# Output layer of a graph-network kernel: four stages a unit apart, two buffers each, bias on GpSimd, last bins first

## The chip, the cores and the metric

The kernel runs on one core of a Trainium2 chip. A core has TensorE (PE, with its weight loads as PEld), VectorE (DVE), ScalarE (ACT), GpSimd (POOL) and SyncE (SP, which here only starts transfers); each takes its instructions in order from a queue of its own. The metric is the device time of one execution in microseconds, smaller is better. `L569` is line 569 of the kernel before the change.

## The reference, cut to what matters

```python
def smu(x, alpha=0.01, mu=2.5):
    return ((1 + alpha) * x + (1 - alpha) * x * erf(mu * (1 - alpha) * x)) / 2

# x (12500, 128), 400000 edges; src is sorted; W_f1 (128, 20), the other weights 128x128
h   = maximum(layernorm(x), 0)
h   = h @ W_in2f.T
Wij = smu(edge_attr_20 @ W_f1.T + b_f1) @ W_f2.T + b_f2        # one row per edge
Wij = Wij * edge_weight[:, None]
agg = segment_sum(h[dst] * Wij, src, num_segments=12500)        # (12500, 128)
out = x + smu(agg @ W_o1.T + b_o1) @ W_o2.T + b_o2              # the output layer
```

## The kernel before

The 12500 nodes are cut into `NB` = 98 bins of 128 rows; the last bin has 84. The edges go through the edge loop in groups of four tiles of 128: filter (two matmuls and a Gelu), gather of `h`, product, and a scatter (L572, GpSimd's indirect DMA) of each edge's message into a buffer in DRAM with room for every bin. The groups are divided into nine epochs with a buffer each. While epoch k is scattered, the buffer of epoch k-1 is read back and summed: `fetch` (L593) loads a chunk of `SPAN[k]` bins into a tile `rw` of 128 x (12 x 129) values, `choose` (L604) makes one-hot matrices `se` from the slot numbers that ride along, `add` (L617) multiplies them on TensorE into a PSUM bank `pg` of four bins, and L630 adds the bank to `agg`, which stays in SBUF, 128 x 12544. Four chunks are fetched ahead (`AHEAD`), in four buffers.

The last epoch has no edge loop beside it. Its buffer, 98 bins of 256 rows, is read in chunks of six bins (`SPAN` = 6, two matmuls a bin) after the last scatter has landed. Around its sums the output layer is computed in 26 units: 24 of four bins, then bin 96 and the 84 rows of bin 97 alone. A unit goes through

- `half`: L228 or L230 loads the unit's old rows of `x` (tile `hg`, 256 KB) from ScalarE's queue; L231 is the first matmul (PSUM `pu`, one bank); L232 the Gelu on ScalarE (`ge`); L233 on VectorE makes `sm` from both;
- `rest`: L239 is the second matmul (PSUM `pw`, one bank, four matmuls of 128 x 128); L240 adds the old rows into `ms`; L241 adds the output bias `bo2`, broadcast over the unit's bins, and L243 or L245 stores `ms` from ScalarE's queue.

The order on PE, DVE, ACT and SP is the order in which the program emits instructions. `half` of a unit is emitted when the four bins behind it have been added (`open_halves`, one unit of delay), and `rest` two bins later (`close_halves`). After the last bin, the remaining three units run one after another. At the end a flag (`nbad`, L830 to L835) is read by all engines; it decides whether a general path, not run here, computes the result anew.

The functions that the change touches, as they were:

Of the kernel before, what the change touches and what calls it, by code (L numbers as in the profile page):

```python
# [9 lines left out]
F32 = mybir.dt.float32  # L10
# [9 lines left out]
P = 128  # L20
# [9 lines left out]
GRP = 4  # L30
# [3 lines left out]
ROW = P + 1  # L34
# [5 lines left out]
def gnn_kernel(  # L40
# [19 lines left out]
    nc = tc.nc  # L60
# [15 lines left out]
    for n in PARTS:  # L76
        n = min(n, left)
# [5 lines left out]
    EPOCHS = len(eps_of)  # L83
# [6 lines left out]
    Q = [c // P for c in CAP]  # L90
    ROWS = 2 * max(Q)
    SPAN = [ROWS // q for q in Q]
# [46 lines left out]
    agg = const.tile([P, NB * P], F32, name="agg")  # L139
# [8 lines left out]
    w_o1 = const.tile([P, P], F32, name="w_o1")  # L148
    w_o2 = const.tile([P, P], F32, name="w_o2")
    bo2 = const.tile([P, P], F32, name="bo2")  # L150
# [69 lines left out]

    units = [(b, n, P) for b, n in chunks(NB - 1, GRP)] + [(NB - 1, 1, LASTB)]

    def half(unit, tiles, po, queue):
        xr, ge, sm, ys = tiles
        b, n, rows = unit
        w = (n - 1) * P + rows
        if rows == P:
            queue.dma_start(xr[:, :n, :], bin_rows(x, b, n))  # L228
        else:
            queue.dma_start(xr[:rows, 0, :], x[b * P:N, :])  # L230
        nc.tensor.matmul(po[:, :w], w_o1, agg[:, b * P:b * P + w], start=True, stop=True)  # L231
        nc.scalar.activation(ge[:, :w], po[:, :w], AF.Gelu, scale=ZS, bias=bz)  # L232
        nc.vector.scalar_tensor_tensor(sm[:, :w], po[:, :w], LIN, ge[:, :w], op0=ALU.mult, op1=ALU.add)  # L233

    def rest(unit, tiles, py, queue):
        xr, ge, sm, ys = tiles
        b, n, rows = unit
        for j in range(n):
            nc.tensor.matmul(py[:rows, j, :], sm[:, j * P:j * P + rows], w_o2, start=True, stop=True)  # L239
        nc.vector.tensor_add(ys[:rows, :n], py[:rows, :n], xr[:rows, :n, :])  # L240
        nc.vector.tensor_add(ys[:rows, :n], ys[:rows, :n], bo2[:rows].unsqueeze(1).to_broadcast([rows, n, P]))  # L241
        if rows == P:
            queue.dma_start(bin_rows(out, b, n), ys[:, :n])  # L243
        else:
            queue.dma_start(out[b * P:N, :], ys[:rows, 0])  # L245


    with tc.tile_pool(name="ld", bufs=4) as ld, \
# [151 lines left out]
        last = {}  # L400
# [182 lines left out]

        rows_in, sel, pgs = {}, {}, {}

        def fetch(k, c):

            b = c * SPAN[k]
            if b >= NB:
                return  # L590
            n = min(SPAN[k], NB - b)
            rw = rowp.tile([P, ROWS, ROW], F32, name="rw")
            nc.sync.dma_start(rw[:, :n * Q[k]].rearrange("p (b q) r -> p b (q r)", b=n),  # L593
                              bufs[k][b * CAP[k]:(b + n) * CAP[k], :].rearrange("(b p q) r -> p b (q r)", b=n, p=P))
            rows_in[c] = rw

        def choose(k, c):

            b = c * SPAN[k]
            if b >= NB:  # L600
                return
            m = min(SPAN[k], NB - b) * Q[k]
            se = rowp.tile([P, ROWS, P], F32, name="se", bufs=2)
            nc.vector.tensor_tensor(se[:, :m], irow_ps.unsqueeze(1).to_broadcast([P, m, P]),  # L604
                                    rows_in[c][:, :m, P:P + 1].to_broadcast([P, m, P]), op=ALU.is_equal)
            sel[c] = se

        def add(k, b, q):

            g = b % GRP  # L610
            c, i = b // SPAN[k], b % SPAN[k]
            if q == 0 and g == 0:
                pgs[0] = ps2.tile([P, GRP, P], F32, name="pg")
            if q == 0 and i == 0:
                choose(k, c + 1)
            o = i * Q[k] + q
            nc.tensor.matmul(pgs[0][:, g, :], rows_in[c][:, o, 0:P], sel[c][:, o, :], start=(q == 0),  # L617
                             stop=(q == Q[k] - 1))
            if q < Q[k] - 1:
                return  # L620
            if i == SPAN[k] - 1 or b == NB - 1:
                rows_in.pop(c), sel.pop(c)
                fetch(k, c + AHEAD)
            if g == GRP - 1 or b == NB - 1:
                dst = agg[:, (b - g) * P:(b + 1) * P]
                src = pgs[0][:, :g + 1].rearrange("p b n -> p (b n)")
                if k == 0:
                    nc.vector.tensor_copy(dst, src)
                else:
                    nc.vector.tensor_add(dst, dst, src)  # L630

        AHEAD = 4

        def begin(k):
            for c in range(AHEAD):
                fetch(k, c)

        def parts(k, upto):
            nonlocal done
            while done < upto:  # L640
                add(k, *work[done])
                done += 1
# [90 lines left out]
        for g in range(NG):  # L733
            s = g // PER
            k = epoch[s]
            g0, ng = eps_of[k][0] * PER, min(eps_of[k][1] * PER, NG - eps_of[k][0] * PER)
            i = g - g0
# [46 lines left out]
            assert k == 0 or taken_steps == COUNT and next(h_steps, None) is None  # L784
        k = EPOCHS - 1
        begin(k)
        choose(k, 0)
        mids, ends = [], []
        units_in = {}
        for unit in units:  # L790
            units_in.setdefault(unit[0] // GRP, []).append(unit)

        def open_halves(last):
            while mids and (last or len(mids) > 1):
                for unit in units_in[mids.pop(0)]:
                    tiles = (edge.tile([P, GRP * P], F32, name="hg").rearrange("p (b d) -> p b d", b=GRP),
                             edge.tile([P, GRP * P], F32, name="ge"),
                             edge.tile([P, GRP * P], F32, name="sm"),
                             msg.tile([P, GRP, ROW], F32, name="ms")[:, :, 0:P])
                    half(unit, tiles, ps1.tile([P, GRP * P], F32, name="pu"), nc.scalar)  # L800
                    ends.append((unit, tiles))
                    if last:
                        close_halves()

        def close_halves():
            while ends:
                unit, tiles = ends.pop(0)
                rest(unit, tiles, ps1.tile([P, GRP, P], F32, name="pw"), nc.scalar)

        for b in range(NB):  # L810
            for q in range(Q[k]):
                add(k, b, q)
            if b % GRP == 1:
                close_halves()
            if b % GRP == GRP - 1 or b == NB - 1:
                mids.append(b // GRP)
                open_halves(False)
        close_halves()
        open_halves(True)

    with tc.tile_pool(name="fps", bufs=1, space=PSUM) as fps:
        ends = const.tile([P, 2], F32, name="ends")
# [13 lines left out]
    with tc.If(flag > 0):  # L836
        with tc.tile_pool(name="gl", bufs=1) as gl, tc.tile_pool(name="gps", bufs=1, space=PSUM) as gps:
# [11 lines left out]
            with tc.For_i(0, NT, 1) as t:  # L849
# [11 lines left out]
                hg = gl.tile([P, D], F32, name="ghg")  # L861
# [39 lines left out]
            for b, n in chunks(NB, GRP):  # L901
                pt = gps.tile([P, GRP * P], F32, name="gpt")
                w = min(N, (b + n) * P) - b * P
                for j in range(n):
                    rows = min(P, N - (b + j) * P)
# [3 lines left out]
                nc.vector.tensor_copy(agg[:, b * P:b * P + w], pt[:, :w])  # L909
        with tc.tile_pool(name="gfin", bufs=1) as fin, tc.tile_pool(name="gfps", bufs=1, space=PSUM) as fps:  # L910
            for unit in units:
                tiles = (fin.tile([P, GRP, P], F32, name="xr"), fin.tile([P, GRP * P], F32, name="fge"),
                         fin.tile([P, GRP * P], F32, name="fsm"), fin.tile([P, GRP, P], F32, name="ys"))
                half(unit, tiles, fps.tile([P, GRP * P], F32, name="gpo"), nc.sync)
                rest(unit, tiles, fps.tile([P, GRP, P], F32, name="gpy"), nc.sync)


# [46 lines left out]
```

## Time and profile before

| | |
|---|---|
| median of 3 runs | 4244.77 us (4242.52 to 4252.45) |
| profiled execution, its own time | 4248.45 us |
| its span in the trace | 4246.6 us, mean granted clock 0.969 |
| busy over the span | PE 3736.8 (88%), DVE 3220.9 (76%), POOL 3017.8 (71%), ACT 2830.2 (67%) |
| last scatter issued (L572) | 4068.9 us |
| first fetch of the last epoch issued (L593) | 4071.28 us |
| first Gelu of the output layer (L232) | 4085.23 us |
| last VectorE instruction (L241) | starts 4241.59 us |

Times in the profile's views are microseconds from the span's start. A group's row has its line, engine, operation, output and inputs with shapes, the count, busy time, mean ns of one, and after the bar the idle time of the engine before these instructions with what ended it. A wait for several things is put down to the one that came last; where the engine named had long been done, it was another. ACTq and SPq mark instructions that start a transfer. Matmuls in f32 appear as two instructions each.

### The profile page before, as it was taken

To read this page: it belongs to the slowest core of one execution; us is meant where nothing else is said; L and a number is where in the kernel's file an instruction comes from. 1 tells how busy PE (TensorE), PEld (TensorE's weight loads), DVE (VectorE), ACT (ScalarE), POOL (GpSimd) and SP (SyncE) were. 2 spreads that over 40 slices of the span, in tenths; PEclk is the share of its full clock that TensorE was granted. 3 is DMA by queue.
4 is the path that set the end of the run, shared out by engine and by line. 5 is a ranking of instruction groups with operands and counts; after the bars stand their busy time and mean duration, and the time that the engine had idled before them with its cause. 6 is when DMAs were issued, how large, how long until landed. Compare 5 with 4: busy or idle time off the path is not lost. (4 is left out here: it accounts for less than half of the span.)

```text
span 4246.6 us, 74532 instructions
## 1 busy us (share of the span) xinstructions
PE 3736.8 (88%) x18497; PEld 2320.1 (55%) x18794; DVE 3220.9 (76%) x8578; ACT 2830.2 (67%) x11057; POOL 3017.8 (71%) x3133
## 2 busy tenths in 40 slices
PE   5877788999988999979998979998999799898976
PEld 2334434655555655546555546665666566565755
DVE  5886777877767877768877768887888688787865
ACT  4777777776666767657766757776777576676621
POOL 3777777777777777777777777777777777777620
PEclk9999999999999999989999989999999999999988
DMA  7855665766647666756666657775899699786754
GB/s 216 227 148 162 180 173 179 210 205 193 200 145 217 206 197 204 199 156 202 213 196 199 179 176 205 215 214 167 231 231 235 188 246 233 209 233 177 206 165 122
DMA packets 512380, 834.71 MB, mean 197 GB/s; under 512 B 84576, under 2 KB 323398, under 8 KB 511810
## 3 DMA queue, kind: packets, MB, share of 16 engines
q1 hardware_dynamic: 380986, 601.70, 51.8%
q0 software_dynamic: 100000, 206.60, 15.8%
q10 hardware_dynamic: 30952, 21.54, 1.8%
q8 instruction: 152, 2.49, 0.3%
q14 instruction: 290, 2.38, 0.2%
HBM read 456.16 MB, written 373.36 MB: 195 GB/s over the span
## 5 line engine op out<-in xcount | busy, mean ns | idle before, releaser
L572 POOL DMA_INDIRECT buf<-ms,ix x3125 | 3016.8, 965 | 1051.5 <-issue 249.2
L617 PEld LDWEIGHTS pg<-se,rw 128*128 128x128 f32 x8036 | 1096.5, 193 | 158.6 <-issue 21.2
L569 ACT ACTIVATE ms<-pt,w_sb 128x128 f32<-128x128 f32 x3125 | 905.1, 391 | 342.3 <-DMA buf<-ms,ix 163.6
L617 PE MATMUL pg<-se,rw 128*128 128x128 f32 x8036 | 1118.7, 276 | 10.4 <-DVE se L604 10.4
L467 ACT ACTIVATE jk<-pc,nbig 128x98 f32<-128x98 f32 x3125 | 1027.7, 351 | 6.1 <-PE pc L438 5.4
L539 PE MATMUL pw<-sm,w_f 128*128 128x512 f32 x1564 | 883.5, 647 | 40.6 <-DVE sm L505 35.4
L549 DVE SCALAR_TENSOR_TENSOR mt<-pw,b,hg 128x512 f32<-128x512 f32 x782 | 582.8, 745 | 348.2 <-ACT hg L528 345.9
L497 ACT ACTIVATE ge<-pu 128x512 f32<-128x512 f32 x782 | 468.4, 599 | 558.8 <-PE pu L489 537.0
L489 PE MATMUL pu<-f,w_f 128*128 128x512 f32 x1564 | 812.3, 601 | 4.2 <-DVE sm L505 4.1
L559 PE MATMUL pt<-ident,mt 128*128 128x128 f32 x3125 | 495.3, 281 | 298.8 <-DVE mt L549 295.8
L604 DVE TENSOR_TENSOR se<-irow_ps,rw 128x1536 f32<-128x1536 f32 (+1 forms) x345 | 587.5, 1703 | 145.8 <-DMA rw<-buf 125.2
L505 DVE SCALAR_TENSOR_TENSOR sm<-pu,ge 128x512 f32<-128x512 f32 x782 | 535.0, 684 | 209.7 <-ACT ge L497 200.8
L467 ACT ACTIVATION_READ_ACCUMULATOR jk<-pc,nbig 128x1 f32 x3125 | 674.5, 216 | 0.0
L528 ACT ACTIVATE hg<-ph 128x512 f32<-128x512 f32 x782 | 469.1, 600 | 305.3 <-PE ph L520 303.8
L520 PE MATMUL ph<-oh,hw 128*128 128x512 bf16 (+1 forms) x2049 | 631.8, 387 | 16.1 <-issue 0.4
L559 PEld LDWEIGHTS pt<-ident,mt 128*128 128x128 f32 x3125 | 352.9, 142 | 389.7 <-DVE mt L549 382.5
L424 DVE TENSOR_TENSOR co<-co,po 128x98 f16<-128x98 f16 x2353 | 502.6, 214 | 81.1
L520 PEld LDWEIGHTS <-hw 128*128 128x128 bf16 x2346 | 232.9, 99 | 553.6 <-issue 453.7
L410 DVE TENSOR_TENSOR po<-irow_ps,hi_b 128x392 f16<-128x392 f32 x782 | 433.1, 554 | 0.0
L539 PEld LDWEIGHTS pw<-sm,w_f 128*128 128x128 f32 x1564 | 236.8, 191 | 169.7 <-DVE sm L505 164.7
L489 PEld LDWEIGHTS pu<-f,w_f 128*128 128x128 f32 x1564 | 253.6, 196 | 27.9 <-DVE sm L505 5.6
L437 PE MATMUL pc<-co,ones_h 128*128 128x392 f16 x782 | 258.3, 330 | 3.5 <-DVE co L424 3.5
(104 smaller groups left out, 1702.0 us busy)
## 6 DMA issues: line engine op xcount, KB each, us to landing
rw<-buf SPq DMA_DIRECT2D x292, 774.0 KB
rbc<-rel_dram SPq DMA_DIRECT2D x390, 256.0 KB
buf<-zero SPq DMA_DIRECT2D x243, 387.0 KB
buf<-ms,ix POOLq DMA_INDIRECT x3125
buf<-zero SPq DMA_DIRECT2D x193, 258.0 KB
hw<-h_dram SPq DMA_DIRECT2D x391, 96.0 KB
rw<-buf SPq DMA_DIRECT2D x49, 645.0 KB
f<-in_f_t SPq DMA_DIRECT2D x390, 80.0 KB
```

The costliest lines, as they stand in the source:

```text
L424: nc.vector.tensor_add(co[:, j], co[:, j - 1], po[:, j - 1])
L467: nc.scalar.activation(jk, pc[:, j], AF.Relu, bias=nbig, accum_out=sl[:, j:j + 1])
L489: nc.tensor.matmul(pu[:, :n], w_f1, loaded[g // PER][0][:, o:o + n], start=True, stop=True)
L505: nc.vector.scalar_tensor_tensor(sm[:, :n], units_of.pop(g)[:, :n], LIN, hidden[g][:, :n], op0=ALU.mult, op1=ALU.add)
L520: nc.tensor.matmul(ph[:, :n], hw[:, q * D:(q + 1) * D], oh[:, o:o + n], start=(q == 0), stop=(q == 2))
L539: nc.tensor.matmul(pw[:, :n], w_f2, hidden.pop(g)[:, :n], start=True, stop=True)
L549: nc.vector.scalar_tensor_tensor(mt[:, :n], pws.pop(g)[:, :n], b2, rows_of.pop(g)[:, :n], op0=ALU.add, op1=ALU.mult)
L559: nc.tensor.transpose(pt[:, j, :], mt[:, j * P:(j + 1) * P], ident)
L569: nc.scalar.activation(ms[:, j, 0:P], pt[:, j], AF.Copy, scale=w_sb[:, t + j:t + j + 1])
L572: i = nc.gpsimd.indirect_dma_start(out=bufs[k][:, :], out_offset=bass.IndirectOffsetOnAxis(ap=ix[:, j:j + 1], axis=0), in_=ms[:, j, :], in ...
L604: nc.vector.tensor_tensor(se[:, :m], irow_ps.unsqueeze(1).to_broadcast([P, m, P]), rows_in[c][:, :m, P:P + 1].to_broadcast([P, m, P]), op= ...
L617: nc.tensor.matmul(pgs[0][:, g, :], rows_in[c][:, o, 0:P], sel[c][:, o, :], start=(q == 0), stop=(q == Q[k] - 1))
```

## The change

The output layer of the last epoch is cut into four steps that are emitted a unit or half a unit apart: `first_half` (first matmul and Gelu), `between` (`sm`), `second_half` (second matmul) and `store` (sum with the old rows, and the store). The matmul results take turns in two banks each, `pu`/`ph` and `pw`/`pt`, tiles that the edge loop has used. The old rows are loaded four units ahead, in turns into `hg` and `mt` with two buffers each, still from ScalarE's queue; GpSimd adds the output bias to them in place, and L241 is gone. The stores go into SP's queue, where the fetches are. The last chunk of bins (96 and 97) comes first in the last epoch, and the two small units with it; the order of the other epochs stays.

```diff
+    def with_bias(unit, xr, engine):
+        b, n, rows = unit
+        engine.tensor_add(xr[:rows, :n], xr[:rows, :n], bo2[:rows].unsqueeze(1).to_broadcast([rows, n, P]))
...
-    def rest(unit, tiles, py, queue):
-        xr, ge, sm, ys = tiles
+    def rest(unit, sm, py):
         b, n, rows = unit
         for j in range(n):
             nc.tensor.matmul(py[:rows, j, :], sm[:, j * P:j * P + rows], w_o2, start=True, stop=True)
+
+    def stored(unit, py, xr, ys, queue):
+        b, n, rows = unit
         nc.vector.tensor_add(ys[:rows, :n], py[:rows, :n], xr[:rows, :n, :])
-        nc.vector.tensor_add(ys[:rows, :n], ys[:rows, :n], bo2[:rows].unsqueeze(1).to_broadcast([rows, n, P]))
...
+        order_of = []
+        for k in range(EPOCHS):
+            cs = list(range(-(-NB // SPAN[k])))
+            order_of.append(cs if k < EPOCHS - 1 else cs[-1:] + cs[:-1])
...
-        mids, ends = [], []
...
+        small = [u for u in units if u[0] >= NB // GRP * GRP]
+        row_of, ready, opened, smoothed, summed = [], [], [], [], []
+        wanted = small + [u for u in units if u not in small]
+
+        def ask():
+            if wanted:
+                unit = wanted.pop(0)
+                name = ("hg", "mt")[len(wanted) % 2]
+                xr = edge.tile([P, GRP * P], F32, name=name).rearrange("p (b d) -> p b d", b=GRP)
+                old_rows(unit, xr, nc.scalar)
+                with_bias(unit, xr, nc.gpsimd)
+                row_of.append((unit, xr))
...
+        def first_half():
+            unit = ready.pop(0)
+            po = ps1.tile([P, GRP * P], F32, name=other(0, ("pu", "ph")))
+            ge = edge.tile([P, GRP * P], F32, name="ge")
+            half(unit, po, ge)
+            opened.append((unit, po, ge))
+
+        def between():
+            unit, po, ge = opened.pop(0)
+            sm = edge.tile([P, GRP * P], F32, name="sm")
+            bent(unit, po, ge, sm)
+            smoothed.append((unit, sm))
+
+        def second_half():
+            unit, sm = smoothed.pop(0)
+            py = ps1.tile([P, GRP, P], F32, name=other(1, ("pw", "pt")))
+            rest(unit, sm, py)
+            summed.append((unit, py))
+
+        def store():
+            unit, py = summed.pop(0)
+            was, xr = row_of.pop(0)
+            assert was == unit
+            stored(unit, py, xr, msg.tile([P, GRP, ROW], F32, name="ms")[:, :, 0:P], nc.sync)
+            ask()
+
+        for _ in range(4):
+            ask()
+        for c in order_of[k]:
+            for b in range(c * SPAN[k], min(NB, (c + 1) * SPAN[k])):
+                for q in range(Q[k]):
+                    add(k, b, q)
+                if b % GRP == 1:
+                    if opened:
+                        between()
+                    if summed:
+                        store()
+                if b % GRP == GRP - 1 or b == NB - 1:
+                    ready += [u for u in units if u[0] // GRP == b // GRP]
+                    if smoothed:
+                        second_half()
+                    if len(ready) > 1:
+                        first_half()
+        while ready or opened or smoothed or summed:
+            if smoothed:
+                second_half()
+            if ready:
+                first_half()
+            if opened:
+                between()
+            if summed:
+                store()
```

In the changed kernel the bias add on GpSimd is L236, the sum with the old rows L254, the first matmul, Gelu and `sm` are L240, L241 and L245, the second matmul L250, the stores L256 and L258, `choose` L627, the adds L640 and the sum into `agg` L653.

More of the change, by code (lines that the diff above doesn't have):

```diff
@@ L221, in gnn_kernel, with width, old_rows @@
     units = [(b, n, P) for b, n in chunks(NB - 1, GRP)] + [(NB - 1, 1, LASTB)]
-    def half(unit, tiles, po, queue):
-        xr, ge, sm, ys = tiles
+    def width(unit):
         b, n, rows = unit
-        w = (n - 1) * P + rows
+        return (n - 1) * P + rows
+    def old_rows(unit, xr, queue):
+        b, n, rows = unit
         if rows == P:
@@ L230, in half, with bent @@
             queue.dma_start(xr[:rows, 0, :], x[b * P:N, :])
-        nc.tensor.matmul(po[:, :w], w_o1, agg[:, b * P:b * P + w], start=True, stop=True)
+    def with_bias(unit, xr, engine):
+        b, n, rows = unit
+        engine.tensor_add(xr[:rows, :n], xr[:rows, :n], bo2[:rows].unsqueeze(1).to_broadcast([rows, n, P]))
+    def half(unit, po, ge):
+        w = width(unit)
+        nc.tensor.matmul(po[:, :w], w_o1, agg[:, unit[0] * P:unit[0] * P + w], start=True, stop=True)
         nc.scalar.activation(ge[:, :w], po[:, :w], AF.Gelu, scale=ZS, bias=bz)
+    def bent(unit, po, ge, sm):
+        w = width(unit)
         nc.vector.scalar_tensor_tensor(sm[:, :w], po[:, :w], LIN, ge[:, :w], op0=ALU.mult, op1=ALU.add)
-    def rest(unit, tiles, py, queue):
-        xr, ge, sm, ys = tiles
+    def rest(unit, sm, py):
         b, n, rows = unit
@@ L239, in rest @@
             nc.tensor.matmul(py[:rows, j, :], sm[:, j * P:j * P + rows], w_o2, start=True, stop=True)
+    def stored(unit, py, xr, ys, queue):
+        b, n, rows = unit
         nc.vector.tensor_add(ys[:rows, :n], py[:rows, :n], xr[:rows, :n, :])
-        nc.vector.tensor_add(ys[:rows, :n], ys[:rows, :n], bo2[:rows].unsqueeze(1).to_broadcast([rows, n, P]))
         if rows == P:
@@ L584, in gnn_kernel, with behind @@
         rows_in, sel, pgs = {}, {}, {}
+        order_of = []
+        for k in range(EPOCHS):
+            cs = list(range(-(-NB // SPAN[k])))
+            order_of.append(cs if k < EPOCHS - 1 else cs[-1:] + cs[:-1])
+        def behind(k, c, n):
+            i = order_of[k].index(c) + n
+            return order_of[k][i] if i < len(order_of[k]) else None
         def fetch(k, c):
+            if c is None:
+                return
             b = c * SPAN[k]
-            if b >= NB:
-                return
             n = min(SPAN[k], NB - b)
@@ L597, in choose @@
         def choose(k, c):
+            if c is None:
+                return
             b = c * SPAN[k]
-            if b >= NB:
-                return
             m = min(SPAN[k], NB - b) * Q[k]
@@ L614, in add @@
             if q == 0 and i == 0:
-                choose(k, c + 1)
+                choose(k, behind(k, c, 1))
             o = i * Q[k] + q
@@ L622, in add @@
                 rows_in.pop(c), sel.pop(c)
-                fetch(k, c + AHEAD)
+                fetch(k, behind(k, c, AHEAD))
             if g == GRP - 1 or b == NB - 1:
@@ L634, in begin @@
         def begin(k):
-            for c in range(AHEAD):
+            for c in order_of[k][:AHEAD]:
                 fetch(k, c)
@@ L786, in gnn_kernel @@
         begin(k)
-        choose(k, 0)
-        mids, ends = [], []
[L789 to L819, printed above, removed]
+        choose(k, order_of[k][0])
@@ new lines, in gnn_kernel, with other @@
+        turns = [0, 0]
+        def other(i, names):
+            turns[i] += 1
+            return names[turns[i] % 2]
+        def first_half():
[9 more added lines that the diff above has]
+            smoothed.append((unit, sm))
@@ L911, in gnn_kernel @@
             for unit in units:
[L912 to L915, printed above, removed]
+                xr, ys = fin.tile([P, GRP, P], F32, name="xr"), fin.tile([P, GRP, P], F32, name="ys")
+                ge, sm = fin.tile([P, GRP * P], F32, name="fge"), fin.tile([P, GRP * P], F32, name="fsm")
+                po, py = fps.tile([P, GRP * P], F32, name="gpo"), fps.tile([P, GRP, P], F32, name="gpy")
+                old_rows(unit, xr, nc.sync)
+                with_bias(unit, xr, nc.vector)
+                half(unit, po, ge)
+                bent(unit, po, ge, sm)
+                rest(unit, sm, py)
+                stored(unit, py, xr, ys, nc.sync)
 def arrange(inputs):
```

## The prediction

> **What bounds the kernel now.** I read first the busy time by stretch, to find the stage that the change touches. Columns: stretch and length, then busy us of PE, PEld, DVE, ACT and POOL, the granted clock, DMA share, GB/s.
>
> ```profile
> 4040.00:4060.00 20.00, 19.72 (x129) 15.03 (x129) 17.08 (x37) 12.39 (x48) 14.47 (x16) 1.00 0.49 149
> 4060.00:4080.00 20.00, 8.69 (x63) 8.09 (x64) 7.31 (x17) 1.68 (x6) 7.67 (x8) 0.75 0.54 169
> 4140.00:4160.00 20.00, 14.10 (x81) 11.62 (x80) 11.33 (x14) 2.06 (x3) 0.00 (x0) 0.84 0.55 158
> ```
>
> Until 4060 the edge loop keeps TensorE at 98%. Its instruction order is the same in both kernels, so nothing before 4065 should move. From 4067 on there is only the last epoch with the output layer: 180 of the 4246.6 us, in which no engine is full, GpSimd is idle, the clock is 0.84 and the DMA share 0.55. No engine bounds this stage; a chain does. Next the groups and the waits of 4084 to 4232, where 24 full units run (23 inside for some lines):
>
> ```profile
> L617 PE MATMUL pg<-se,rw 128*128 128x128 f32 x363 | 53.6, 296 | 0.0
> L239 PE MATMUL pw<-w_o,sm 128*128 128x128 f32 x186 | 30.7, 315 | 47.2 <-DVE sm L233 47.2
> L604 DVE TENSOR_TENSOR se<-irow_ps,rw 128x1536 f32<-128x1536 f32 (+1 forms) x15 | 25.2, 1677 | 1.0 <-PE pg L617 1.0
> L233 DVE SCALAR_TENSOR_TENSOR sm<-pu,ge 128x512 f32<-128x512 f32 x24 | 16.6, 690 | 21.1 <-ACT ge L232 21.1
> L232 ACT ACTIVATE ge<-pu,bz 128x512 f32<-128x512 f32 x24 | 16.5, 687 | 148.9 <-DVE agg L630 83.7 <-PE pu L231 56.2 <-DVE se L604 4.5
> L630 DVE TENSOR_TENSOR agg<-agg,pg 128x512 f32<-128x512 f32 (+1 forms) x24 | 16.0, 666 | 0.0
> L241 DVE TENSOR_TENSOR ms<-ms,bo 128x512 f32<-128x512 f32 x23 | 15.9, 692 | 0.8
> L240 DVE TENSOR_TENSOR ms<-pw,hg 128x512 f32<-128x512 f32 x23 | 15.9, 691 | 40.3 <-DMA hg<-in_x 26.0 <-PE pw L239 14.3
> ```
>
> TensorE loses 47.2 us, all waiting for `sm`; `sm` waits for the Gelu `ge`; and `ge` names `agg` L630, which it does not read. What holds `ge` is seen in one unit of the timeline (start, duration, idle before):
>
> ```profile
> 4129.73 0.52 ACTq L228 DMA_DIRECT2D hg<-in_x  x1
> ...
> 4133.77 1.02 PE L231 MATMUL pu<-agg,w_o 128*128 128x512 f32 x2
> ...
> 4135.43 0.69 DVE L240 TENSOR_TENSOR ms<-pw,hg 128x512 f32<-128x512 f32 x1 [2.00 <-DMA hg<-in_x]
> 4136.15 0.69 DVE L241 TENSOR_TENSOR ms<-ms,bo 128x512 f32<-128x512 f32 x1
> ...
> 4136.88 0.39 ACTq L243 DMA_DIRECT2D out<-ms  x1
> 4137.31 0.52 ACTq L228 DMA_DIRECT2D hg<-in_x  x1
> 4137.93 0.69 ACT L232 ACTIVATE ge<-pu,bz 128x512 f32<-128x512 f32 x1 [6.89 <-DVE agg L630]
> 4138.65 0.69 DVE L233 SCALAR_TENSOR_TENSOR sm<-pu,ge 128x512 f32<-128x512 f32 x1 [1.21 <-ACT ge L232]
> ...
> 4139.49 2.05 PE L239 MATMUL pw<-w_o,sm 128*128 128x128 f32 x8 [3.80 <-DVE sm L233]
> ```
>
> ScalarE's queue is a loop: the load of the old rows, 5.7 us until L240 can use them, L240, L241, the store's issue behind L241, the next load, and only then the next `ge`, though `pu` was ready at 4134.79. That is 7.58 us from load to load (4129.73 to 4137.31). Other units take 5.4. From the second load (4089.84) to the 24th (4229.37) the mean is 139.5/22 = 6.34 us a unit. After the 3.8 us of idle the eight L239 take 2.05 us instead of 1.13: the idle also costs TensorE its clock.
>
> **The change, part by part.** Off the loop: the store leaves ScalarE's queue for SP's, the loads run four units ahead in two tiles of two buffers, the bias add L241 (0.69) leaves VectorE, and `pu`/`ph` and `pw`/`pt` give each matmul result two banks. No step waits for a transfer just issued any more. What sets the pace next?
>
> TensorE packed: start to start in the trace, second half 0.97 (4146.60 to 4147.57), eight adds 0.89 (to 4148.46), first half 0.86 (to 4149.32), eight adds 0.89: 3.61 us a unit at full clock.
>
> VectorE and the order: for three units (12 bins, two `choose`) it has 3 x (`sm` 0.69 + add 0.69 + `agg` 0.68) + 2 x 1.75 = 9.7 us, below 3 x 3.61 = 10.8, but in a fixed order. I step through it with the adds of a unit starting at 0, 0.04 for a hand-over and 0.2 for the matmul's drain. Unit B: adds from 3.61, `ge` 3.82 to 4.51, `sm` to 5.24, add to 5.95, `choose` to 7.72, `agg` to 8.42; its second half starts on time at 5.39. Unit C: adds from 7.22, `ge` done 8.12, `sm` 8.44 to 9.13, so the second half starts at 9.19 instead of 9.0. Next unit: `agg` to 10.54, `choose` to 12.31, `sm` to 13.02, the second half at 13.08 instead of 12.8. The cycle repeats after 11.3 us: 3.77 a unit.
>
> ScalarE: `ge` 0.69 and one load issue, 0.39 to 0.52, waiting for VectorE's add; in those steps it ends over 0.8 us before the next `ge` is due. SP takes 26 stores of some 0.39 = 10 us. SP waited 111.9 us for TensorE between 4070 and 4247, so the issue time is free; but a store waits there for L254, and a fetch stands behind it. A fetch is used by `choose` about two chunks (11.3 us) after its issue, and one VectorE instruction of delay doesn't use that up. Each transfer also waits for the eighth before it; eight are three units' worth, again 11.3 us. The longer waits are off the path unless DMA gets slow.
>
> DMA: 98 bins x 132 KB = 12.9 MB in, 6.4 MB old rows, 6.4 MB out. The four fetches alone ran at 99.8% share and 313 GB/s (4072 to 4080, start included). In 4084 to 4232 the old rows and stores used 28.1% of 148 us for 12.04 MB, 3.45 us a MB, and the rest 24.8% for 9.78 MB, 3.75. At these, 12.9 x 3.75 + 12.8 x 3.45 = 92.5 us of full DMA. The stage below lasts about 105 us: DMA hides, at 88% share against 55%. This is the thinnest cover in the sum; I add 4 us for it (0 to 20).
>
> GpSimd: 26 adds of 128x512 f32 in L236. No such row is in the trace. Nearest by shape: L241, 0.69 on VectorE; nearest on the engine: L572, 0.97. The Trainium skill (GPSIMD Engine Reference, section 3.1) speaks against this move: a two-input add there is priced 1.96 times VectorE's, 4497 ns at 2048 elements, some 6 us more at the first call of newly loaded code. I take 0.69 x 1.96 = 1.36 us, an estimate; unscaled 4.5 is the upper end. With 1.36 it sits in a unit of 3.77 and its load is issued four units ahead: 15 us, less 5.7 for landing. By trace or rule alike it costs nothing; at 4.5 it would set the pace: 25 x 4.5 = 113 us. The first four stand behind the last scatter (4068.9), and 6 us of loading would end before the first is wanted at about 4084.
>
> Ports: the same skill (SBUF — State Buffer, Who interferes with whom) says that a VectorE instruction with two SBUF inputs and a GpSimd one that reads SBUF block each other for the whole instruction. In the trace GpSimd does no adds, so no row shows it. Of the rows above only L241 reads two SBUF tiles, and it goes; the others read one PSUM and one SBUF tile. By the rule the sum stays; if they did block, 1.36 a unit on VectorE (3.23 busy) makes 4.6 a unit: +20 us.
>
> Last bins first, start: fetches still wait for the last scatter (4071.28). The two-bin chunk (258 KB) should land near 4074 rather than 4075.84; its adds run on a cold clock to 4076.3. `choose` of chunk 0 follows to about 4078.6, so the first full unit starts 1 us later than now (4077.70). Its 16 adds take 3.3 us cold (0.207 each, from 32 in 6.64), then the two small units and a half-warm unit: I put the third full unit at 4086.7. The last adds begin 21 units later, 4086.7 + 21 x 3.77 = 4165.9, and end at 4167.7.
>
> The end: in the same steps, `ge`, `sm`, second half and add of the last two units take 7.0 us to 4174.7. Now it is 4224.9 to 4241.9, 17.0, because three units, two of them small, go one after another. From the last VectorE instruction to the end of the span are 4.7 us now; the last store is 256 KB instead of 42, +0.8. SP reads the flag ahead of the last store; on SP a register read with its checks fits in the 0.97 us between the issues of L385 and L388, and the flag is ready 1 us early: 0 (up to 1).
>
> Sum: 4174.7 + 4.7 + 0.8 + 4 for DMA = 4184.2, against a span of 4246.6: -62.4. The execution's own time is 4248.45, 1.85 outside the span, so 4186.1 for one like it. The median of the runs is 4244.77, 3.7 lower: 4182.4, rounded 4183.
>
> **Rivals.** (1) DMA becomes the bound: 25 MB at 200 to 215 GB/s, like the busier slices of the edge loop, instead of 240: 117 to 125 us from 4072.8 and 2.4 to the end: span 4192 to 4201. For: 512-byte rows both ways and 88% share. Against: slices of 106 us at 246 GB/s, and four chunks of prefetch. VectorE would wait for `rw`, as L604 does only at 4075 now. (2) GpSimd and VectorE block each other: the +20 above, 4204, and up to 4215 with the DMA allowance doubled. (3) Slower than before: the add in L236 works by rows of the broadcast operand, four short pieces for one, each with the 0.97 of a GpSimd instruction plus 0.8 of work: 7.1 us a unit. Then 25 x 7.1 = 178 from 4070 and 7 to the end: 4255 span, +8. It decides above 6.7 us an add. Against: L241 takes the same broadcast at the plain price. (4) The change doesn't shorten the loop because `ge` still waits for a transfer: only if the loads aren't ahead; they are issued in ScalarE's order four units early. Then -17 + 7 at the end: 4237.
>
> **Numbers.** Engine pace as summed 0.58 (4176 to 4192); DMA 0.25 (4192 to 4204); blocking 0.08 (4204 to 4215); unchanged loop 0.04; GpSimd slow 0.05. About 0.3% (13 us) is what a measurement of this kernel can tell from no change. The first three are faster: 0.91; the loop case about same: 0.04; slower 0.05. The range takes the first three, with PE packed without waits (24 x 0.16 = 4 less, no DMA allowance) as lower end: spans of 4176 to 4215, medians 1.8 lower: 4174 to 4213.
>
> **What would show it.** Right: second half to second half near 3.8 us, clock 1.00 from 4090, `ge` released by its own matmul, no wait of L254 for POOL, DMA share near 0.85, last adds near 4168 and 7 us after them. Wrong: `choose` or L254 waiting for DMA, L236 above 3.8 us, VectorE rows longer than 0.69 while GpSimd adds, a clock below 0.95, or the edge loop ending elsewhere than 4067.

## The result and the profile after

The changed kernel takes 4176.18 us, the median of 4 runs (4174.89 to 4181.54), against 4245.53 for the kernel before in the same comparison: ratio 0.9835, 95% interval [0.9822, 0.9848]. The prediction was 4183 in a range of 4174 to 4213. The profiled execution takes 4181.54, with a span of 4179.2 instead of 4246.6. One trace read below, that of e2, is of a slow execution (5317.66 us, against 5233.76 to 5272.49 for the others of e2), though the granted clock in the stage read from it is 1.00; the ratios are of fast executions alone.

The edge loop ends where it did. The first fetch of the last epoch is issued at 4071.5 (before: 4071.3), and from it to the end of the span are 107.7 us instead of 175.3: all of the difference lies in this stage. Busy time by stretch (stretch and length, busy us of PE, PEld, DVE, ACT and POOL, granted clock, DMA share, GB/s):

```profile
4060.00:4080.00 20.00, 9.53 (x65) 8.66 (x66) 7.47 (x19) 1.97 (x7) 10.94 (x12) 0.81 0.61 187
4100.00:4120.00 20.00, 20.00 (x143) 17.01 (x142) 16.08 (x20) 4.12 (x6) 7.65 (x6) 1.00 0.98 281
4140.00:4160.00 20.00, 20.00 (x143) 16.97 (x142) 16.08 (x21) 4.12 (x6) 7.64 (x6) 1.00 0.78 227
```

In 4140 to 4160 TensorE was busy for 14.10 of 20 us at a clock of 0.84; now it is busy for all of them at 1.00. The DMA share is up from 0.55 to 0.78, and to 0.98 in an earlier stretch, and TensorE has no idle time even there. The groups of 4084 to 4164 (busy us and mean ns of one, then idle us before it and its releasers):

```profile
L640 PE MATMUL pg<-se,rw 128*128 128x128 f32 x360 | 43.9, 275 | 0.0
L250 PE MATMUL pt<-w_o,sm 128*128 128x128 f32 x88 | 12.4, 284 | 0.0
L627 DVE TENSOR_TENSOR se<-irow_ps,rw 128x1536 f32<-128x1536 f32 x14 | 24.5, 1750 | 0.0
L245 DVE SCALAR_TENSOR_TENSOR sm<-pu,ge 128x512 f32<-128x512 f32 x11 | 7.6, 692 | 7.9 <-ACT ge L241 7.3
L241 ACT ACTIVATE ge<-pu,bz 128x512 f32<-128x512 f32 x11 | 7.6, 687 | 32.5 <-PE pu L240 32.5
L254 DVE TENSOR_TENSOR ms<-pt,mt 128x512 f32<-128x512 f32 (+1 forms) x11 | 7.1, 646 | 0.0
L236 POOL TENSOR_TENSOR mt<-mt,bo 128x512 f32<-128x512 f32 x11 | 14.0, 1275 | 40.3 <-DMA mt<-in_x 35.8 <-DVE se L627 2.7 <-DVE agg L653 1.0
```

The second matmul, which lost 47.2 us to `sm`, shows no idle time any more. The Gelu waits for its own matmul and no longer shows `agg`, which it does not read. `choose` (L627) and the sum (L254) have no idle time in front of them, so neither the fetches, nor the old rows, nor GpSimd's add is late. GpSimd itself waits 35.8 us for the old rows in this group; that is idle time of an engine with time to spare. The chain that ended last is TensorE alone until 4166.4 (start, duration, what):

```profile
4149.97 1.00 PE pw L250 x8
4150.97 0.86 PE ph L240 x2
4151.83 1.78 PE pg L640 x16
4153.61 1.00 PE pt L250 x8
```

1.00 + 0.86 + 1.78 = 3.64 us: that is the pace of a unit, and by this view all of it is TensorE's. The timeline shows a second limit at the same place (start, duration; in brackets the idle time before):

```profile
4131.61 1.13 PE L250 MATMUL pt<-w_o,sm 128*128 128x128 f32 x8
...
4132.57 1.02 PE L240 MATMUL pu<-agg,w_o 128*128 128x512 f32 x2
...
4133.70 0.69 ACT L241 ACTIVATE ge<-pu,bz 128x512 f32<-128x512 f32 x1 [2.96 <-PE pu L240]
4134.42 0.69 DVE L245 SCALAR_TENSOR_TENSOR sm<-pu,ge 128x512 f32<-128x512 f32 x1
4135.02 0.68 DVE L254 TENSOR_TENSOR ms<-pt,mt 128x512 f32<-128x512 f32 x1
...
4135.26 1.13 PE L250 MATMUL pw<-w_o,sm 128*128 128x128 f32 x8
...
4135.73 0.37 SPq L256 DMA_DIRECT2D out<-ms  x1
4135.74 0.47 ACTq L230 DMA_DIRECT2D mt<-in_x  x1
```

From one second half to the next are 3.65 us, and the steps between them touch: first half 0.96 later, Gelu 1.13 after it, `sm` 0.72 later, second half 0.84 after that. `sm` ends at 4135.11, 0.15 us before its matmul, and so in each of the 22 units from 4087 on. That is no slack: where TensorE is seen to wait for `sm`, as in e7 below with 0.41 us of idle time, its matmul also starts 0.15 us after `sm` ends. So TensorE is full, and the chain from one second half over the first half, the Gelu and `sm` to the next is just as long. In e3 below, 16 of 22 units follow each other at 3.58 or 3.59 us with the same matmuls, so TensorE's own work is some 0.06 us below the pace. The store and the next load are issued last, side by side on two queues, and neither TensorE nor VectorE waits for them.

### The profile page after: what moved, and what is told of

It reads as the page before. It is cut to its first block, busy times and chain, and to the rows that moved or that the text cites. A ratio compares the mean times of both kernels' runs of the same rounds, so it can differ in the third digit from the quotient of the medians.

```text
span 4179.2 us, 74603 instructions
## 1 busy us (share of the span) xinstructions
PE 3714.5 (89%) x18497; PEld 2304.1 (55%) x18794; DVE 3199.9 (77%) x8552; ACT 2828.3 (68%) x11057; POOL 3053.1 (73%) x3159
## 3 DMA queue, kind: packets, MB, share of 16 engines
q0 software_dynamic: 100000, 206.60, 16.1%
q14 instruction: 290, 2.38, 0.2%
## 5 line engine op out<-in xcount | busy, mean ns | idle before, releaser
L640 PEld LDWEIGHTS pg<-se,rw 128*128 128x128 f32 x8036 | 1087.7, 192 | 152.9 <-issue 14.4
L640 PE MATMUL pg<-se,rw 128*128 128x128 f32 x8036 | 1109.0, 275 | 7.9 <-DVE se L627 7.9
L627 DVE TENSOR_TENSOR se<-irow_ps,rw 128x1536 f32<-128x1536 f32 (+1 forms) x345 | 587.5, 1703 | 149.6 <-DMA rw<-buf 129.2
```

## The experiments

All numbers of a stage below are taken the same way: its length from the first fetch of the last epoch to the end of the span, and the mean time from one Gelu to the next over full units 2 to 23. e1 to e4 ran on one chip and e5 to e8 on another, and on both the whole program takes about 1 ms more (kernel before: 5287.61 and 5287.15 us); each ratio is to the kernel before on the same chip. There the executions of the kernel before alone lie between 5269.73 and 5320.59 us, so a time of one run prices nothing, and the prices below are differences between stages, from one trace each. The changed kernel was not traced on those chips. Its stage is set beside theirs because rows of the same shape last equally long (in e6 as here the Gelu 0.69, `choose` 1.75, GpSimd's add 1.27 us). Two stretches of the stage differ with edits that do not touch them: from the first fetch to the first add 3.6 us in the changed kernel and 5.4 in e5 and e8, from the end of the last VectorE instruction to the end of the span 8.0 in the changed kernel and 6.0 in e7 and e8. A difference of 2 us between two stages is therefore no price, and the time a unit is the surer reading.

| kernel | stage us | us a unit | time us | ratio to before |
|---|---|---|---|---|
| before | 175.3 | 6.40 | 4245.53 | |
| before, rows asked four ahead (e1) | 155.0 | 5.55 | 5278.82 | 0.9968 [0.9941, 0.9995] |
| before, stores in SP's queue (e2) | 136.0 | 4.84 | 5265.42 | 0.993 [0.9895, 0.9965] |
| changed, two steps as before (e4) | 131.0 | 4.59 | 5231.7 | 0.9887 [0.9836, 0.9938] |
| changed, one bank each (e5) | 123.8 | 4.18 | 5229.94 | one run |
| changed, rows one unit ahead (e3) | 116.4 | 3.89 | 5239.27 | 0.9876 [0.9832, 0.9919] |
| changed, bias on both engines (e8) | 116.2 | 3.99 | 5224.62 | one run |
| changed, bias on VectorE (e7) | 114.4 | 3.96 | 5271.97 | one run |
| changed, bins in order (e9) | 109.1 | 3.64 | 4178.12 | one run |
| **changed** | **107.7** | **3.65** | **4176.18** | **0.9835 [0.9822, 0.9848]** |
| changed, stores in ScalarE's queue (e6) | 106.6 | 3.69 | 5230.66 | one run |
| changed, warm start and other last stores (e10) | 104.8 | 3.65 | 4173.36 | 0.9829 [0.9816, 0.9843] |
| changed, four GpSimd adds a unit (e11) | 143.4 | 4.75 | 4216.66 | one run |

**One part alone, on the kernel before.** e1 takes the load out of the loop in ScalarE's queue, e2 the store.

```diff
 e1
+        for _ in range(4):
+            ask()                       # old rows into hg/mt, from nc.scalar
...
                 rest(unit, tiles, ps1.tile([P, GRP, P], F32, name="pw"), nc.scalar)
+                ask()
 e2
-                rest(unit, tiles, ps1.tile([P, GRP, P], F32, name="pw"), nc.scalar)
+                rest(unit, tiles, ps1.tile([P, GRP, P], F32, name="pw"), nc.sync)
```

> The kernel before with one edit: the old rows are loaded four units ahead into hg and mt, still from ScalarE's queue; stores, bias, banks, steps and order as before. Theory (the loop load, sum, bias, store issue, next load, Gelu on ScalarE's queue set the pace): the load leaves the loop, but the store still stands ahead of the next Gelu: second half 0.97, L240 and L241 to 2.4, store issue to 3.0, Gelu to 3.7, sm to 4.4 (5.4 where a choose comes first): about 4.8 us a unit instead of 6.3, span about 4210, the end (17 us from the last add) unchanged. Rival (the spacing of the steps is what costs, not the queue): pace stays above 5.8, span above 4234.

> The kernel before with one edit: the stores are started from SP's queue; loads, bias, banks, steps and order as before. Theory: with the store gone from ScalarE's queue, each load is started right behind the Gelu of the unit before, a unit early, by itself; pace 4.5 to 4.8, span about 4208, as with the rows ahead, since either edit opens the same loop. Rival (stores in SP's queue hold up the fetches): choose waits for rw, span above 4246. Rival (the spacing costs): span above 4234.

e1 came out at 5.55 us a unit, not at the 4.8 expected, and e2 at 4.84, just above its 4.5 to 4.8; that either edit opens the same loop is refuted. The timeline of e1 (its lines are numbered otherwise: L237 Gelu, L246 bias, L248 store, L226 load):

```profile
5161.99 0.69 DVE L246 TENSOR_TENSOR ms<-ms,bo 128x512 f32<-128x512 f32 x1
...
5162.72 0.39 ACTq L248 DMA_DIRECT2D out<-ms  x1
5163.15 0.52 ACTq L226 DMA_DIRECT2D hg<-in_x  x1
...
5163.77 0.69 ACT L237 ACTIVATE ge<-pu,bz 128x512 f32<-128x512 f32 x1 [4.79 <-PE pg L622]
...
5165.33 1.13 PE L244 MATMUL pw<-w_o,sm 128*128 128x128 f32 x8 [1.71 <-DVE sm L238]
```

The landing time is gone, the loop is not. The store still waits for the bias add of this unit, and behind the store stand the load's issue and the next unit's Gelu, although the Gelu's input was ready by about 5162.8 (L236 begins at 5161.71 and takes 1.02). One unit's sum is still ahead of the next unit's Gelu. In e2 it is not (L243 store, L228 load, L232 Gelu):

```profile
5230.98 0.37 SPq L243 DMA_DIRECT2D out<-ms  x1
5231.09 0.69 ACT L232 ACTIVATE ge<-pu,bz 128x512 f32<-128x512 f32 x1 [3.85 <-PE pu L231]
5231.17 0.37 ACTq L228 DMA_DIRECT2D hg<-in_x  x1
```

One word of the change opens the loop: the Gelu is released by its own matmul, and the load follows it a unit early, with no rows asked ahead. The stage falls by 175.3 - 136.0 = 39.3 us, twice what the loads alone bring (20.3). The times agree: 0.993 is 37 us, with an interval of 18 to 56, and for e1 it is 17 us, 3 to 31. What keeps e2 at 4.84 is for the most part the two-step order: from 5195 to 5295 TensorE still loses 21.5 us to `sm` (us in total, times, longest), and e4 below, which has all of the change but the four steps, stands at 4.59.

```profile
PE pw L239 <- DVE sm L233: 21.5, 20, 1.8
```

**The changed kernel with one part undone.** e4 goes back to two steps a unit (the Gelu and `sm` issued with the first matmul, the sum and the store with the second). e5 gives each matmul result one bank.

```diff
 e4                                                   # at b % GRP == 1
-                    if opened:
-                        between()
-                    if summed:
+                    if smoothed:
+                        second_half()
                         store()
...
-                    if smoothed:
-                        second_half()
                     if len(ready) > 1:
                         first_half()
+                        between()
 e5
-            po = ps1.tile([P, GRP * P], F32, name=other(0, ("pu", "ph")))
+            po = ps1.tile([P, GRP * P], F32, name="pu")
...
-            py = ps1.tile([P, GRP, P], F32, name=other(1, ("pw", "pt")))
+            py = ps1.tile([P, GRP, P], F32, name="pw")
```

> The changed kernel with one edit: the four steps are put back into the two of before (first half and sm together after the fourth bin, second half and store together after the second); queues, rows ahead, GpSimd bias, banks and order as changed. Theory: TensorE waits for sm again: first half ends 2.0 after the second half began, Gelu 2.9 to 3.6, sm to 4.3 or, behind a choose, 4.8: pace 4.4 to 4.6 instead of 3.65, span about 4201. Rival (only queues and prefetch matter): pace below 3.8, span 4179 to 4184.

> The changed kernel with one bank for each matmul result again (pu and pw only). Read by the stage from the last epoch's first fetch to the end (175.3 us before, 107.7 changed) and the pace of the Gelus (6.40, 3.65). Theory: pu in one bank costs nothing, since the first half of the next unit stands behind the second half, which needs sm; pw in one bank makes each second half wait for L254, which starts 0.6 after sm and ends 0.5 after the second half could begin: pace about 4.15, stage about 119. Rival (the banks are idle cover): pace 3.65, stage 108.

Both came out at the pace that was expected; the stage of e5, 123.8, is longer than the 119, and 1.8 us of that are a later first add. In e4 the waits of 5110 to 5205 (engine, tile and line, releaser, us in total, times, longest) name the step that is missing:

```profile
ACT ge L241 <- PE ph L240: 42.8, 11, 4.2
PEld pt L250 <- DVE sm L245: 9.8, 10, 1.2
PEld pw L250 <- DVE sm L245: 9.8, 10, 1.2
```

The Gelu is on time, but only eight adds stand between the first half and the second, and TensorE waits about 1 us for `sm` in every unit. The four steps are worth 131.0 - 107.7 = 23.3 us (19.7 of them from the second full Gelu to the 23rd), once the rest is there; alone on the kernel before they were not run. In e5 the second half waits for the sum of the unit before it, because it writes the bank that the sum reads:

```profile
5164.53 0.68 DVE L254 TENSOR_TENSOR ms<-pw,hg 128x512 f32<-128x512 f32 x1
...
5165.26 1.16 PE L250 MATMUL pw<-w_o,sm 128*128 128x128 f32 x8 [0.38 <-DVE ms L254]
```

That is 0.38 us of idle time 21 times, and 0.53 us a unit in all. The stage is 16.1 us longer, of which 11.2 lie in the same part (87.8 against 76.6): so much is shown for the second banks. Which of the two pairs it is was not tried apart; the waits name `pw`.

e3 asks for the rows of one unit at the start instead of four; e6 puts the stores back into ScalarE's queue; e9 leaves the bins in their order.

```diff
 e3
-        for _ in range(4):
-            ask()
+        ask()
 e6
-            stored(unit, py, xr, msg.tile([P, GRP, ROW], F32, name="ms")[:, :, 0:P], nc.sync)
+            stored(unit, py, xr, msg.tile([P, GRP, ROW], F32, name="ms")[:, :, 0:P], nc.scalar)
 e9
-        wanted = small + [u for u in units if u not in small]
+        wanted = list(units)
...
-            order_of.append(cs if k < EPOCHS - 1 else cs[-1:] + cs[:-1])
+            order_of.append(cs)
```

> The changed kernel with one edit: one unit's old rows asked for at the start instead of four, so that each load is issued only after the unit before has used its rows. Theory: a loop comes back, load to landing 5.2, GpSimd 1.27, sum 0.68, issue: 7.3 us a unit instead of 3.65, span about 4179 + 24 x 3.65 = 4267, slower than before, with the Gelu no longer waiting behind a store but the store step waiting for GpSimd. Rival (the steps and banks carry the gain): pace below 5, span below 4215.

> The changed kernel with the stores back in ScalarE's queue. Theory: in the four-step order the store's wait for L254 ends 1.4 us after a Gelu and the next Gelu is due 2.9 after it; store issue 0.4 and load issue 0.5 fit between: pace stays 3.65, and as SP is free of the last store the end after the last VectorE instruction falls from 8.0 towards 5: stage 104 to 108. Rival (a store in ScalarE's queue costs by itself, as the 39 us of the store edit alone suggest): pace 4.5 or more, stage 125 or more.

> The changed kernel with the bins of the last epoch in their natural order, the two small units last. Theory (the order is worth little: the first two bins and the two small units run for nothing while the first fetches land): the first full adds come 1 us earlier, but the end has two more steps of a chain, some 1.3 us each, and TensorE has some 2 us of adds and small matmuls more after 4079: stage 109 to 112 instead of 107.7, pace 3.65. Rival (no effect): 107 to 108.5.

The expectation of e3 fell. It had the loop come back at 7.3 us a unit; 3.89 was measured, and the kernel is still faster than before. In the timeline of e3:

```profile
5160.35 0.69 ACT L241 ACTIVATE ge<-ph,bz 128x512 f32<-128x512 f32 x1 [2.90 <-PE ph L240]
5160.41 0.37 ACTq L230 DMA_DIRECT2D mt<-in_x  x1
5160.56 0.69 DVE L254 TENSOR_TENSOR ms<-pt,mt 128x512 f32<-128x512 f32 x1 [2.38 <-POOL mt L236]
```

The load at 5160.41 does not wait for the sum at 5160.56 that stands ahead of it in the program, because with four buffers it overwrites nothing that is still to be read. It is issued right behind the Gelu, a unit early. Some units wait all the same, L254 here for 2.38 us: its own rows were asked for at 5153.25, 1.15 us behind a fetch, and GpSimd could start on them only at 5159.26. Asking four ahead is worth 116.4 - 107.7 = 8.7 us, 5.2 of them from the second full Gelu to the 23rd, and it is not what opens the loop.

e6 shows that the queue of the stores, which decides on 39 us in the kernel before, hardly matters any more: 106.6 us. The Gelu now stands a unit ahead of the store in the program, so the store at 5183.48 delays only the load at 5183.96, and the next Gelu is not due until 5185.08:

```profile
5183.48 0.39 ACTq L256 DMA_DIRECT2D out<-ms  x1
...
5183.96 0.47 ACTq L230 DMA_DIRECT2D hg<-in_x  x1
...
5185.08 0.69 ACT L241 ACTIVATE ge<-pu,bz 128x512 f32<-128x512 f32 x1 [2.96 <-PE pu L240]
```

The pace is 3.69 instead of 3.65 because two loads take 1.60 and 1.32 us to issue and hold up a Gelu each; the end behind the last VectorE instruction is 2.1 us shorter. So another queue and another order are alternatives for the loop, and of the two only the order can also close TensorE's gap, together with the second banks (e5) and the bias (e7). e9 is 1.4 us longer: its first full Gelu comes 1.6 us earlier after the fetch and its last VectorE instruction 2.1 us later, as expected in kind, and the end behind that is 0.7 us shorter. One trace each does not tell such a difference from none.

**The bias.** e7 puts it back on VectorE, as a second add behind the sum. e8 leaves GpSimd's add in place and has VectorE add zeros there, so that VectorE does an instruction with two SBUF inputs beside GpSimd's. e11 has GpSimd add zeros three times more.

```diff
 e7, e8                                               # bo2 in e7, zeros in e8
         nc.vector.tensor_add(ys[:rows, :n], py[:rows, :n], xr[:rows, :n, :])
+        nc.vector.tensor_add(ys[:rows, :n], ys[:rows, :n], bo2[:rows].unsqueeze(1).to_broadcast([rows, n, P]))
...
-                with_bias(unit, xr, nc.gpsimd)       # gone in e7 only
 e11
-        engine.tensor_add(xr[:rows, :n], xr[:rows, :n], bo2[:rows].unsqueeze(1).to_broadcast([rows, n, P]))
+        for more in (bo2, zero[:, 0:P], zero[:, 0:P], zero[:, 0:P]):
+            engine.tensor_add(xr[:rows, :n], xr[:rows, :n], more[:rows].unsqueeze(1).to_broadcast([rows, n, P]))
```

> The changed kernel with the bias added on VectorE behind L254, as before, and nothing on GpSimd. Theory: VectorE's instructions follow each other at 0.60 to 0.61 us, choose at 1.67: four of the one and two thirds of the other make 3.54 a unit, just under 3.65; pace 3.65 to 3.9, stage 108 to 114. Rival (relief of VectorE is a main part of the gain): pace 4.2 or more, stage above 121.

> The changed kernel, GpSimd's bias add kept, with one VectorE instruction more behind L254 that adds zeros (two SBUF inputs, shape of the old bias add). Theory (the two engines block each other where VectorE reads two SBUF tiles): the added rows that meet a GpSimd add last up to 0.69 + 1.27 = 2.0 us, or the GpSimd rows grow from 1.27 to as much; pace above that of the kernel with the bias on VectorE alone by 0.1 to 0.5. Rival (no blocking): rows stay at 0.69 and 1.27 whether they meet or not, and the pace is that of the kernel with the bias on VectorE.

> The changed kernel with three GpSimd adds of zeros more for each unit (four of 1.27 = 5.1 us instead of one). Theory (one add has cover up to the pace of 3.65, beyond it GpSimd sets the pace): pace 5.1 to 5.3, stage 107.7 + 24 x 1.5 = about 143, VectorE's rows unchanged at 0.68 to 0.69 as each reads one SBUF tile. Rival (the four units of rows ahead absorb it): pace 3.65 for most units, stage below 120.

e7 is a little slower than expected, 3.96 a unit: the longer row of VectorE instructions makes `sm` late (start, duration, idle time before):

```profile
5207.36 0.68 DVE L245 SCALAR_TENSOR_TENSOR sm<-pu,ge 128x512 f32<-128x512 f32 x1
...
5208.19 1.02 PE L250 MATMUL pw<-w_o,sm 128*128 128x128 f32 x7 [0.41 <-DVE sm L245]
```

The move to GpSimd is worth 6.7 us of the stage, 6.5 of them from the second full Gelu to the 23rd. e8 shows where the ports matter (L255 is the added instruction, L236 GpSimd's):

```profile
5164.77 0.69 DVE L255 TENSOR_TENSOR ms<-ms,zero 128x512 f32<-128x512 f32 x1
5164.78 1.82 POOL L236 TENSOR_TENSOR mt<-mt,bo 128x512 f32<-128x512 f32 x1 [1.44 <-DVE ms L254]
...
5175.15 1.27 POOL L236 TENSOR_TENSOR mt<-mt,bo 128x512 f32<-128x512 f32 x1 [4.91 <-DMA mt<-in_x]
5175.47 0.68 DVE L245 SCALAR_TENSOR_TENSOR sm<-pu,ge 128x512 f32<-128x512 f32 x1
...
5176.38 1.27 POOL L236 TENSOR_TENSOR hg<-hg,bo 128x512 f32<-128x512 f32 x1
...
5176.79 1.41 DVE L255 TENSOR_TENSOR ms<-ms,zero 128x512 f32<-128x512 f32 x1
```

At 5164.77 VectorE is first by 0.01 us, and GpSimd takes 1.82 instead of 1.27. At 5176.79 GpSimd has been at an add since 5176.38, and VectorE's 0.69 becomes 1.41. Of the 26 added instructions 10 meet a GpSimd add; six of the 10 are themselves longer, 0.82 to 1.41 us, and each of these ends 0.54 to 0.55 us after GpSimd's add; two make GpSimd's add longer; two overlap it by 0.15 us at most and change nothing. The `sm` at 5175.47 runs inside a GpSimd add and takes its usual 0.68: it reads one PSUM and one SBUF tile. That is the rule of the Trainium skill that the prediction weighed (SBUF — State Buffer, Who interferes with whom), now with its numbers. It costs little. The pace, 3.99, is 0.03 above that of e7 and not the 0.1 to 0.5 expected, and of the 1.8 us between the stages 1.7 lie before the first add.

e11 makes GpSimd the bound. The stage, 143.4, is what was expected; the mean pace of the Gelus, 4.75, is not, since the first units run ahead of GpSimd. Groups of 4090 to 4190, then waits of the same stretch:

```profile
L237 POOL TENSOR_TENSOR mt<-mt,zero 128x512 f32<-128x512 f32 x30 | 38.1, 1269 | 2.4
```

```profile
DVE ms L255 <- POOL hg L237: 15.9, 8, 2.6
DVE ms L255 <- POOL mt L237: 13.7, 7, 2.6
```

Four adds of 1.27 are 5.1 us a unit. The first seven units still run at 3.65, on the rows asked ahead; the rest take 5.26, as expected of all, and VectorE's sum waits for GpSimd. The kernel takes 4216.66 us, still less than before. In the changed kernel, one add of 1.27 in a unit of 3.65 leaves GpSimd idle for two thirds of it.

**A version beyond the change.** e10 takes two losses that the trace after still shows. TensorE stands idle for 7.9 us while the first fetch lands, and its clock is then 0.50 from 4074 to 4080, so eight matmuls into an unused tile keep it busy there; and the last three stores go to ScalarE's queue.

```diff
         choose(k, order_of[k][0])
+        for _ in range(8):
+            idle = ps1.tile([P, GRP * P], F32, name="pc")
+            nc.tensor.matmul(idle, ident, w_sb[:, 0:GRP * P], start=True, stop=True)
...
-            stored(unit, py, xr, msg.tile([P, GRP, ROW], F32, name="ms")[:, :, 0:P], nc.sync)
+            stored(unit, py, xr, msg.tile([P, GRP, ROW], F32, name="ms")[:, :, 0:P],
+                   nc.sync if len(row_of) > 2 else nc.scalar)
```

> The changed kernel with two additions: eight matmuls of constants into an unused bank (512 columns each) keep TensorE busy between the edge loop and the last epoch's first adds, and the last three stores go through ScalarE's queue, so that SP passes the flag's branch early. Theory: the first 16 full adds take 1.8 us instead of 3.4 (clock 1.00 instead of 0.5), and the end after the last VectorE instruction falls from 8.0 to about 6: stage 103.5 to 105 instead of 107.7, time 3 us (0.07%) below the changed kernel. Rival for the start (the first adds wait for fetch and choose anyway): 107.7 - 2 = 105.7. The adds' start stays within 0.3 us of 8.0 after the fetch.

The first 16 adds of a full unit, in the changed kernel and then in e10:

```profile
4079.46 3.43 PE L640 MATMUL pg<-se,rw 128*128 128x128 f32 x16
```

```profile
4064.17 9.31 PE L813 MATMUL pc<-w_sb,ident 128*128 128x512 f32 x16
4073.32 1.05 PE L640 MATMUL pg<-se,rw 128*128 128x128 f32 x8
...
4076.15 1.95 PE L640 MATMUL pg<-se,rw 128*128 128x128 f32 x16
```

They take 1.95 instead of 3.43 us, at a clock of 1.00. From the last VectorE instruction to the end of the span are 6.3 us instead of 8.0, though e7 and e8 end as early with their stores in SP's queue (see the end, below). The stage is 2.9 us shorter. The time, 4173.36, beats the kernel before clearly (0.9829); against the changed kernel the two intervals overlap, so the 2.9 us are shown by the trace and not by the times.

## Why the prediction was right, and which terms were off

The mechanism holds: the loop in ScalarE's queue opens, TensorE is full at full clock, and DMA, GpSimd and the ports stay hidden. The predicted span was 4184.2, the measured one is 4179.2. The median, 4176.18, lies at the lower end of the range and of the 4176 to 4192 that were given 0.58. Its terms:

| term | predicted | measured | difference |
|---|---|---|---|
| 21 units of the pace | 21 x 3.77 = 79.2 | 21 x 3.646 = 76.6 | -2.6 |
| allowance for DMA | 4 | 0 | -4.0 |
| adds of the third full unit begin | 4086.7 | 4086.0 | -0.7 |
| the last adds | 1.8 | 2.0 | +0.2 |
| end of the last adds to the end of the last VectorE instruction | 7.0 | 6.6 | -0.4 |
| from there to the end of the span | 5.5 | 8.0 | +2.5 |

They add up to -5.0: 7.7 us too much and 2.7 too little, so that a part of the nearness is luck. The rest of the 6.8 us between 4183 and 4176.18 comes from the way from the span to the median: the profiled execution stands 5.4 us above its median where the prediction took 3.7 (1.7 more), its time outside the span is 2.35 where it took 1.85 (0.5 less), and it rounded up by 0.6.

- **The pace.** The step that failed is VectorE's order. It was stepped through with durations, 0.69 and 1.75, plus a hand-over, and had `sm` 0.2 to 0.3 late in two of three units. In the trace two adjacent instructions start 0.60 apart (4134.42 and 4135.02): the next one starts before the last has ended. `sm` starts 0.03 us after its Gelu has ended in each of the 22 units, so VectorE's order delays nothing. The 0.04 us between TensorE's 3.61, which the paragraph before had, and the 3.65 measured fits the hand-over from `sm` to the second half. e7 shows that nothing was left over: one more instruction a unit, and `sm` is 0.41 late.
- **DMA.** The allowance of 4 us was not used. The share was 0.89 at 258 GB/s from 4084 to 4164, where 88% was predicted, and reached 0.98 at 281, and no `choose` in this stretch waited for rows. The first rival, DMA as the bound, had 200 to 215 GB/s for this; it fell on that number.
- **GpSimd.** The add was estimated at 1.36 us from the skill's ratio (GPSIMD Engine Reference, section 3.1) and measured at 1.27, 1.84 times VectorE's 0.69. The price read without scaling, 4.5, and the slow rival's 7.1 are far off. No 6 us of loading show either (that figure stands in section 2.1 of the page, not in 3.1): the first adds take 0.47, 0.46, 1.26 and 1.25 us.
- **Ports.** As argued, none of the rows that are left reads two SBUF tiles, and none is lengthened: `sm`, sum and `agg` take 0.68 to 0.69 and `choose` 1.75 whether GpSimd adds or not. e8 shows that the blocking is real for those that do.
- **The loop.** The prediction let the store, the loads four ahead and the bias leave the loop together, without a price for each. Apart, the store is worth 39.3 us (e2), the loads 20.3 (e1), and in the changed kernel the loads are worth 8.7 (e3) and the stores' queue next to nothing (e6). The rival in which the loop stays because the loads are not ahead is refuted by e3.
- **The end.** The last term, 4.7 + 0.8, was mis-sized by 2.5 us. SP does read the flag ahead of the last store, as was said; what the sum put at nothing is its branch over the fallback, which now stands behind that store. SP's waits on itself, of 4070 to 4180 (us in total, times, longest):

```profile
SPq L900 <- SPq L900: 5.3, 2, 3.3
```

The first lasts 3.3 us from the branch at 4171.6, the second 2.0 us, from 4175.1 to 4177.1. In the kernel before SP reached its branch at 4229.6, 17 us before the end of the span, so that whatever it takes there lay beside the last units. Of the two it is the second that counts: the last store lands at 4174.9, so SP could not have finished before that anyway. And the queue of the stores alone does not bring it about. e7 and e8 keep theirs in SP's queue, wait 3.3 us at the branch but not a second time, and end 6.0 us after their last VectorE instruction; the changed kernel, e3, e4, e5, e9 and e11 have the second wait, of 2.0 to 2.3 us. Why is open.

## What to carry to other kernels

Where an engine's first unit of idle time is put down to a tile that the instruction does not read, follow its queue in program order: here a store's issue held the next unit's Gelu, and either another queue for the store or an order with the Gelu ahead of it takes that away, while asking for inputs earlier does not. A chain of hand-overs between four engines is then shortened by giving each step its own place a stage apart and each result a second bank; step through it with the distances between starts, not with durations, and do not take the time of a hand-over for slack. What was hidden beside the old end of the program comes into view when that end moves up.

## What the hardware showed that was not expected

- The branch at the end. In the changed kernel VectorE stands from 4171.5 to 4174.9 and SP from 4171.6 to 4175.0 and again from 4175.1 to 4177.1. In the kernel before VectorE needed 0.6 us at the same place (4242.2 to 4242.8). In e6, without stores on SP, SP's first wait is 2.7 us and the end comes 5.9 us after the last VectorE instruction. In SP's second wait the only transfers in the trace are three of the kind `instruction`, on queues q8 and q14, so a wait for instructions is possible; no row names what is waited for, and it stays open.
- An instruction with two SBUF inputs that meets a GpSimd add starts on time by the trace and is long: 1.41 instead of 0.69 us on VectorE, 1.42 and 1.82 instead of 1.27 on GpSimd. The wait is inside the row and is not shown as idle time.
- The same program takes 4245 us on one chip and 5287 on two others. The difference lies ahead of the last stage: e6, on one of the two, issues the first fetch of the last epoch at 5122.2 us, the changed kernel on the first chip at 4071.5, and from there they need 106.6 and 107.7. Its cause is open.
